# Per-head weight loads issued from GpSimd's DMA queue instead of SP's

## The chip, the cores and the metric

The kernel runs on one core of a Trainium2 chip. A core has five engines that run their own instruction streams: TensorE (PE, matrix products), VectorE (DVE), ScalarE (ACT), GpSimd (POOL) and SyncE (SP), which here only issues DMAs. An instruction waits on semaphores that other engines or finished DMAs raise, and an engine takes its instructions strictly in order. The metric is device time in microseconds (us): the median of several runs.

## The reference

`L0_attn_x` holds 2048 rows of 256 numbers. What is computed, with D = 256 and 16 heads of 128:

```python
x = x + _layernorm(attn(_layernorm(x)))
x = x + _layernorm(moe(_layernorm(x)))

# attn: every weight is codes * repeat(scales, 32, axis=0)
q, k, v = x @ wq + bq, x @ wk + bk, x @ wv + bv      # 256 -> 2048, 16 heads of 128
scores = einsum('bqhd,bkhd->bhqk', q, k) / sqrt(128)
out = einsum('bhqk,bkhd->bqhd', softmax(scores), v)
return out @ wo + bo

# moe: 8 experts of width 176, the 2 best of each row, weights renormalised
```

A weight is stored as 4-bit style codes (as float32) and one scale per 32 rows and column; the kernel multiplies the two (it "dequantizes").

## The kernel before

The attention part is one loop over `g`, which counts steps. A step is one head `h` (0 to 15) and one tile `t` (0 to 15) of 128 query rows. The instruction order on every engine is the order of the Python code (a manual schedule); the framework adds the semaphore waits.

A step makes the scores of its 128 rows against 2048 keys in two halves (`scores_half`, L447: 12 matmuls of 512 columns, operands split in a high and a low fp16 part, then a maximum on VectorE, L458). ScalarE takes the exponentials of both halves (L469), and one step later normalises them to the high part `ph` in fp16 (L483). VectorE computes the low part `pl` of what fp16 lost (L498), one half in step `g+1`, the other at the start of `g+2`. Both are 128 x 2048 and are transposed by SP-issued DMAs into `pt` (L486 for `ph`, L502 for `pl`). `ph` has three buffers, `pl` two, so a `pl` buffer comes free when its transpose has landed. TensorE multiplies `pt` with V (`pv_part`, L517 to L519) with a lag of 13 half steps, so that the products of four tiles are spread over the four steps after them.

`fill` (L538) adds, in the gaps, the projections of later Q, K and V tiles. Their results go from PSUM through ScalarE into `t32` (two buffers in turn; L204 for Q and K, L235 for V, L530 for the output of a group of four tiles), and GpSimd casts them to a high part and subtracts to get the low part (L205 and L206, L236 and L237, L531 and L532). The output tile `o` is written to HBM from GpSimd's DMA queue (L533).

Weights are handled two heads (a pair) at a time. In even heads below 14, `load_w` fetches the next pair's weights: wv at t=0, wk at t=3, wq at t=6 (L680). One load is five DMAs: four that broadcast a row of scales over 32 partitions each into `st_s` (L130, 64 KB each), and one for the codes into `st_c` (L135, 256 KB). Both staging tiles have one buffer. `dequant` (L148), at the end of steps t=2, 5 and 8, scales and multiplies on GpSimd (L152, L154). In the program's order a load stands at the very start of its step, ahead of that step's `pl` transpose (in `low_half(1)`) and `ph` transpose, all of them on SP's queue. Head 14 loads parts of `wo` instead (`load_wo`, scales from ScalarE's queue and codes from SP's).

After the loop come the output projection and the expert layers, which the change leaves alone.

Of the kernel before, what the change touches and what calls it, by code (L numbers as in the profile page):

```python
# [37 lines left out]
def sandwich(  # L38
# [22 lines left out]
    nc = tc.nc  # L61
# [53 lines left out]
    stage = proj_ctx.enter_context(tc.tile_pool(name="stage", bufs=1, side="right"))  # L115
# [4 lines left out]
    def load_w(p, which, pool, eng, sbufs=1):  # L120
        codes, scales = {
            "q": (wq_codes, wq_scales),
            "k": (wk_codes, wk_scales),
            "v": (wv_codes, wv_scales),
        }[which]
        cols = bass.ts(p, 256)
        sc = pool.tile([128, 2, 256], F32, name="st_s", bufs=sbufs)
        sv = scales.rearrange("(kc b) n -> b kc n", b=4)
        for b in range(4):
            eng.dma_start(  # L130
                out=sc[32 * b : 32 * b + 32],
                in_=sv[b : b + 1, :, cols].to_broadcast([32, 2, 256]),
            )
        cd = pool.tile([128, 2, 256], F32, name="st_c", bufs=sbufs)
        eng.dma_start(  # L135
            out=cd, in_=codes.rearrange("(kc p) n -> p kc n", p=128)[:, :, cols]
        )
        raw[(p, which)] = (sc, cd)
# [9 lines left out]
    def dequant(p, which):  # L148
        sc, cd = raw.pop((p, which))
        f = sig[:, 2, IX[which] : IX[which] + 1]  # L150
        if p > 0:
            nc.gpsimd.tensor_scalar(sc, sc, f, 1.0, ALU.mult, ALU.mult)  # L152
        w = wpool.tile([128, 2, 256], BF, name="w" + which)
        nc.gpsimd.tensor_tensor(w, cd, sc, ALU.mult)  # L154
        W[(p, which)] = w
# [18 lines left out]
    def flush():  # L174
        while pending:
            pending.pop(0)()
# [32 lines left out]
    def proj_v(p, t0, n, tag="pj", wide=None):  # L209
        w = W[(p, "v")]  # L210
        ps = proj_psum(tag)
        for j in range(n):
            i = 0
            for kc in range(2):
                for hl in range(2):
                    nc.tensor.matmul(
                        ps[:, bass.ts(j, 256)], xnT[:, t0 + j, hl * 2 + kc, :],
                        w[:, kc, :], start=(i == 0), stop=(i == 3),
                    )
                    i += 1  # L220
        if t0 % 4 == 0:
            V[(p, t0 // 4)] = kqv.tile([128, 2, 4, 256], HP, name="v", bufs=7)
        v = V[(p, t0 // 4)]
        sl = slice(t0 % 4, t0 % 4 + n)
        psv = ps[:, : n * 256].rearrange("p (t d) -> p t d", d=256)
        if wide is None:
            nc.scalar.copy(v[:, 0, sl, :], psv)
            pending.append(lambda: nc.vector.tensor_tensor(
                v[:, 1, sl, :], psv, v[:, 0, sl, :], ALU.subtract
            ))  # L230
        else:
            t32 = wide.tile([128, 512], F32, name="t32")[:, : n * 256].rearrange(
                "p (t d) -> p t d", d=256
            )
            nc.scalar.copy(t32, psv)  # L235
            nc.gpsimd.tensor_copy(v[:, 0, sl, :], t32)  # L236
            nc.gpsimd.tensor_tensor(v[:, 1, sl, :], t32, v[:, 0, sl, :], ALU.subtract)  # L237
# [209 lines left out]
    def scores_half(h, t, half, m):  # L447
        q = Q[(h, t // 4)]
        qc = bass.ts(t % 4, 128)
        s = s_pair()  # L450
        for j in range(2):
            k = K[(h, 2 * half + j)]
            nc.tensor.matmul(s[:, j, :], q[:, 0, qc], k[:, 0, :], start=True, stop=False)  # L453
            nc.tensor.matmul(s[:, j, :], q[:, 0, qc], k[:, 1, :], start=False, stop=False)  # L454
        for j in range(2):
            k = K[(h, 2 * half + j)]
            nc.tensor.matmul(s[:, j, :], q[:, 1, qc], k[:, 0, :], start=False, stop=True)  # L457
        nc.vector.tensor_reduce(m[:, half : half + 1], s, AX.XY, ALU.max)  # L458
        return s

    def negmax(m):
        nc.vector.tensor_scalar(  # L462
            m[:, 2:3], m[:, 0:1], m[:, 1:2], ssc[:, 1:2], ALU.max, ALU.mult
        )

    def softmax(pair, m):
        p = soft.tile([128, S], F32, name="p")
        for i, s in enumerate(pair):
            nc.scalar.activation(  # L469
                p[:, bass.ts(i, 1024)], s,  # L470
                AF.Exp, bias=m[:, 2:3], scale=ssc[:, 0:1], accum_out=m[:, 3 + i : 4 + i],
            )
        return p

    def recip(m):
        nc.vector.tensor_scalar(
            m[:, 5:6], m[:, 3:4], m[:, 4:5], 1.0 / PS, ALU.add, ALU.mult
        )
        nc.vector.reciprocal(m[:, 6:7], m[:, 5:6])

    def high_part(h, t, m, p):
        ph = soft.tile([128, S], HP, name="ph", bufs=3)
        nc.scalar.activation(ph, p, AF.Copy, scale=m[:, 6:7])  # L483
        if t % 4 == 0:
            PT[(h, t // 4)] = pt.tile([128, 4, 32, 128], HP, name="pt")
        nc.sync.dma_start_transpose(  # L486
            out=PT[(h, t // 4)][:, t % 4, 0:16, :], in_=ph
        )
        return ph
# [3 lines left out]
    def low_half(half, h, t, m, p, ph):  # L493
        if half == 0:
            LOW[(h, t)] = soft.tile([128, S], HP, name="pl")
        pl = LOW[(h, t)]
        cs = bass.ts(half, 1024)
        nc.vector.scalar_tensor_tensor(  # L498
            pl[:, cs], p[:, cs], m[:, 6:7], ph[:, cs], ALU.mult, ALU.subtract
        )  # L500
        if half == 1:
            nc.sync.dma_start_transpose(  # L502
                out=PT[(h, t // 4)][:, t % 4, 16:32, :], in_=LOW.pop((h, t))
            )
# [51 lines left out]
    def pv_unit(u):  # L556
        n, e = divmod(u - PVLAG, 8)
        if 0 <= n < 4 * NH:
            pv_part(n // 4, n % 4, 2 * e, 2 * e + 2)
# [68 lines left out]
    def load_oi(b, half, j, tag="kT"):  # L628
        oi = kqv.tile(
            [128, 4, 2, 256], HP, name="oi", tag=tag, bufs={"kT": 8, "v": 7}[tag]  # L630
        )
        nc.sync.dma_start(
            out=oi, in_=ot_d[b][:, 4 * j : 4 * j + 4, :, bass.ts(half, 256)]
        )
        OIN[(b, half, j)] = oi
# [40 lines left out]
    for g in range(NS + 2):  # L676
        h, t = divmod(g, NT)
        live = g < NS
        if live:
            if t in (0, 3, 6) and h % 2 == 0 and h + 2 < NH:  # L680
                load_w(h // 2 + 1, "vkq"[t // 3], stage, nc.sync)
            m = small.tile([128, 8], F32, name="m", bufs=6)
            s0 = scores_half(h, t, 0, m)
            if g == 0:
                proj_v(0, 0, 2)
                proj_v(0, 2, 2, "pv")
        if g == NS:
            load_oi(0, 1, 1)
            load_oi(0, 1, 2)
            load_oi(0, 1, 3)  # L690
        if prev is not None:
            recip(prev[2])
        if prev2 is not None:
            low_half(1, *prev2)
        flush()
        if defer:
            pv_unit(2 * g - 1)
            defer = False
        pv_unit(2 * g)
        if prev is not None:  # L700
            prev = (*prev, high_part(*prev))
        if live:
            s1 = scores_half(h, t, 1, m)
            negmax(m)
            p = softmax((s0, s1), m)
        if prev is not None:
            low_half(0, *prev)
        prev2 = prev
        first = live and (2 * g + 1 - PVLAG) % 8 == 0
        if not first:  # L710
            pv_unit(2 * g + 1)
        if live:
            fill(h, t)
        if first and h == NH - 1:
            defer = True
        elif first:
            pv_unit(2 * g + 1)
        if live:
            prev = (h, t, m, p)
        else:  # L720
            prev = None
        if h % 2 == 0 and t in (2, 5, 8) and h + 2 < NH:
            dequant(h // 2 + 1, "vkq"[t // 3])
        if h == 0 and t in (8, 9):
            tail_consts(t - 8)
        if h == NH - 2 and t in (7, 10, 13):
            load_wo((t - 7) // 3, stage, ("st_s", "st_c"), 1)
        if h == NH - 2 and t in (9, 12, 15):
            dequant_wo((t - 9) // 3)
        if h == NH - 1:  # L730
            late(t)
        if g == NS:
            X1[0] = kqv.tile([128, 4, D], F32, name="x1_0", tag="kT", bufs=8)
            nc.sync.dma_start(out=X1[0], in_=XV[:, 0])
# [440 lines left out]
```

## Time and profile before

| what | value |
|---|---|
| time, median of 3 runs | 1906.27 us (1903.36 to 1906.44) |
| profiled execution: its time / its span | 1909.43 / 1907.6 us |
| busy: PE, DVE, ACT, POOL | 94%, 86%, 72%, 44% |
| mean granted TensorE clock | 0.986 |
| DMA packets on SP's queue (q1) | 321.54 MB, 90.7% of 16 engines |
| DMA packets on GpSimd's queue (q0) | 16.81 MB, 2.9% of 16 engines |
| `load_w`, `st_s` DMAs on SP | 84 of 64 KB, about 0.42 us of issue each |
| `load_w`, `st_c` DMAs on SP | 21 of 256 KB, 0.43 us of issue each |

A group line reads: line, engine, operation, written tile <- read tiles, shapes, count, then busy time and the mean ns of one, then the idle time of the engine just before these instructions and what ended most of it. A wait line reads: engine and line that waited, who ended the wait, total us, times, longest. A timeline line reads: start, duration (us), engine, line, operation, with the idle time before it in brackets. For DMA-issuing instructions of SP the duration is that of the issue, not of the transfer.

### The profile page before, as it was taken

The numbers are of one execution on the slowest core, as the hardware profiler recorded it, in microseconds if no ns is written. First come the engines' busy times: TensorE is split into PE (matmuls) and PEld (weight loads), VectorE is DVE, ScalarE is ACT, GpSimd is POOL, SyncE is SP. The second block draws the span as 40 slices with busy tenths as digits, with TensorE's granted clock in tenths as the row PEclk, the third lists the DMA queues.
The fourth block names the chain that finished last, engine by engine and source line by source line (L and its number), as shares of the span: only waits on it lengthen the run. The fifth ranks groups of instructions, "written<-read, shape, count | busy, mean of one in ns | idle before, by whom it ended". The sixth has DMA issues, their size and how long they took to land. (4 is left out here: it accounts for less than half of the span.)

```text
span 1907.6 us, 25565 instructions
## 1 busy us (share of the span) xinstructions
PE 1799.8 (94%) x8890; PEld 936.9 (49%) x8890; DVE 1633.2 (86%) x2267; ACT 1364.7 (72%) x1730; POOL 843.4 (44%) x788
## 2 busy tenths in 40 slices
PE   7799989999999899989999899989999988899998
PEld 4344444444444344444444444434444433688887
DVE  7899979998999889988998899879999986457566
ACT  5788868887788778878887788778888776123232
POOL 2354455444544454446444544444445423233232
PEclk9999999999999999999999999999999999999999
DMA  3899999999999999999999999999999999992221
GB/s 95 171 194 190 189 184 197 191 185 189 195 191 187 180 196 190 190 185 191 196 190 184 195 194 190 178 183 192 191 188 204 212 219 216 254 241 73 60 71 56
DMA packets 1141409, 342.31 MB, mean 179 GB/s; under 512 B 1070896, under 2 KB 1131520, under 8 KB 1141280
## 3 DMA queue, kind: packets, MB, share of 16 engines
q1 hardware_dynamic: 1132960, 321.54, 90.7%
q0 software_dynamic: 5216, 16.81, 2.9%
q10 hardware_dynamic: 3104, 2.33, 0.4%
q8 instruction: 70, 1.15, 0.2%
q14 instruction: 59, 0.48, 0.1%
HBM read 53.22 MB, written 18.94 MB: 38 GB/s over the span
## 5 line engine op out<-in xcount | busy, mean ns | idle before, releaser
L498 DVE SCALAR_TENSOR_TENSOR pl<-p,m,ph 128x1024 f16<-128x1024 f32 x512 | 731.9, 1430 | 82.4 <-DMA pt<-pl 74.3
L469 ACT ACTIVATE p<-s,m,ssc 128x1024 f32<-128x1024 f32 x512 | 611.8, 1199 | 192.9 <-DVE m L462 168.1
L458 DVE TENSOR_REDUCE m<-s 128x1 f32<-128x1024 f32 x512 | 621.7, 1214 | 20.9 <-PE s L457 20.1
L483 ACT ACTIVATE ph<-p,m 128x2048 f16<-128x2048 f32 x256 | 513.0, 2004 | 116.6 <-issue 65.1
L453 PE MATMUL s<-kT,qT 128*128 128x512 f16 x1024 | 391.1, 382 | 35.6 <-ACT p L469 33.5
L518 PE MATMUL pv<-pt,v 128*128 128x512 f16 x1024 | 391.6, 382 | 31.5 <-DMA pt<-pl 30.3
L517 PE MATMUL pv<-pt,v 128*128 128x512 f16 x1024 | 391.4, 382 | 5.4 <-DMA pt<-ph 4.3
L454 PE MATMUL s<-kT,qT 128*128 128x512 f16 x1024 | 391.3, 382 | 0.0
L519 PE MATMUL pv<-pt,v 128*128 128x512 f16 x1024 | 391.1, 382 | 0.0
L457 PE MATMUL s<-kT,qT 128*128 128x512 f16 x1024 | 307.1, 382 | 0.0
L205 POOL CAST qT<-t 128x512 f16<-128x512 f32 x63 | 83.6, 1328 | 303.3 <-ACT t L204 303.3
L236 POOL CAST v<-t 128x256 f16<-128x256 f32 (+1 forms) x105 | 49.0, 466 | 304.4 <-ACT t L235 304.4
L454 PEld LDWEIGHTS <-qT 128*128 128x128 f16 x1024 | 100.5, 98 | 154.5 <-issue 53.1
L518 PEld LDWEIGHTS <-v 128*128 128x128 f16 x1024 | 100.8, 98 | 153.1 <-issue 23.8
L517 PEld LDWEIGHTS <-v 128*128 128x128 f16 x1024 | 100.9, 99 | 130.8 <-issue 7.8
L519 PEld LDWEIGHTS <-v 128*128 128x128 f16 x1024 | 100.9, 99 | 128.8 <-issue 12.9
L457 PEld LDWEIGHTS <-qT 128*128 128x128 f16 x1024 | 100.8, 98 | 123.0 <-issue 3.6
L237 POOL TENSOR_TENSOR v<-t,v 128x256 f16<-128x256 f32 (+1 forms) x105 | 155.5, 1481 | 8.4
L453 PEld LDWEIGHTS <-qT 128*128 128x128 f16 x1024 | 100.6, 98 | 111.0 <-issue 3.1
L928 POOL TENSOR_TENSOR hh<-sg,hh 128x512 fp32r<-128x512 f32 x42 | 54.5, 1297 | 144.2 <-ACT hh L927 107.6
L927 ACT CAST hh<-sg 128x512 fp32r<-128x512 f32 (+1 forms) x45 | 27.5, 611 | 118.1 <-DVE sg L939 118.0
L206 POOL TENSOR_TENSOR kT<-t,kT 128x512 f16<-128x512 f32 x60 | 104.4, 1739 | 5.1
(178 smaller groups left out, 1956.6 us busy)
## 6 DMA issues: line engine op xcount, KB each, us to landing
oi<-ot_d SPq DMA_DIRECT2D x32, 512.0 KB, 6.1
ot_d<-o POOLq DMA_DIRECT2D x63, 256.0 KB, 4.2
pt<-ph SPq DMA_TRANSPOSE x256, 5.0
pt<-pl SPq DMA_TRANSPOSE x256, 4.8
cu<-ct_d SPq DMA_DIRECT2D x16, 256.0 KB, 3.8
xt<-in_L_attn_x SPq DMA_DIRECT2D x4, 512.0 KB, 4.4
wos<-in_L_attn_wo_scales ACTq DMA_DIRECT2D x32, 64.0 KB, 4.4
woc<-in_L_attn_wo_codes SPq DMA_DIRECT2D x8, 256.0 KB, 3.4
```

Of the source, the lines that this page charges most:

```text
L206: nc.gpsimd.tensor_tensor(t[:, 1, :], t32, t[:, 0, :], ALU.subtract)
L237: nc.gpsimd.tensor_tensor(v[:, 1, sl, :], t32, v[:, 0, sl, :], ALU.subtract)
L453: nc.tensor.matmul(s[:, j, :], q[:, 0, qc], k[:, 0, :], start=True, stop=False)
L454: nc.tensor.matmul(s[:, j, :], q[:, 0, qc], k[:, 1, :], start=False, stop=False)
L457: nc.tensor.matmul(s[:, j, :], q[:, 1, qc], k[:, 0, :], start=False, stop=True)
L458: nc.vector.tensor_reduce(m[:, half : half + 1], s, AX.XY, ALU.max)
L469: nc.scalar.activation(p[:, bass.ts(i, 1024)], s, AF.Exp, bias=m[:, 2:3], scale=ssc[:, 0:1], accum_out=m[:, 3 + i : 4 + i],)
L483: nc.scalar.activation(ph, p, AF.Copy, scale=m[:, 6:7])
L498: nc.vector.scalar_tensor_tensor(pl[:, cs], p[:, cs], m[:, 6:7], ph[:, cs], ALU.mult, ALU.subtract)
L517: nc.tensor.matmul(ps, vh, d[:, :, c, :], start=(c == 0), stop=False)
L518: nc.tensor.matmul(ps, vh, d[:, :, 16 + c, :], start=False, stop=False)
L519: nc.tensor.matmul(ps, vl, d[:, :, c, :], start=False, stop=(c == 15))
```

## The change

The queue that `load_w` is given in the attention loop becomes GpSimd's. Order and positions in the program stay, so the 105 DMAs (21 loads of five) leave SP's stream and stand in GpSimd's stream at the start of steps t=0, 3 and 6 of even heads: at t=3 and t=6 right behind the `dequant` that ended the step before, and at each of the three ahead of the casts that `fill` adds in that step.

```diff
             if t in (0, 3, 6) and h % 2 == 0 and h + 2 < NH:
-                load_w(h // 2 + 1, "vkq"[t // 3], stage, nc.sync)
+                load_w(h // 2 + 1, "vkq"[t // 3], stage, nc.gpsimd)
```

`load_w` passes that queue to all its DMAs:

```python
for b in range(4):
    eng.dma_start(
        out=sc[32 * b : 32 * b + 32],
        in_=sv[b : b + 1, :, cols].to_broadcast([32, 2, 256]),
    )
...
eng.dma_start(out=cd, in_=codes.rearrange("(kc p) n -> p kc n", p=128)[:, :, cols])
```

## The prediction

> **What bounds the kernel now.** I read the page first, then busy time head by head, then the waits of SP's DMA queue, and at the end the timelines of SP, VectorE and GpSimd around single loads. From the page:
>
> ```profile
> q1 hardware_dynamic: 1132960, 321.54, 90.7%
> q0 software_dynamic: 5216, 16.81, 2.9%
> ...
> L498 DVE SCALAR_TENSOR_TENSOR pl<-p,m,ph 128x1024 f16<-128x1024 f32 x512 | 731.9, 1430 | 82.4 <-DMA pt<-pl 74.3
> ...
> ot_d<-o POOLq DMA_DIRECT2D x63, 256.0 KB, 4.2
> ```
>
> q1 is SP's queue: 512 transposes of 512 KB each fill most of it. L498 writes `pl`, which has two buffers, and waits 74.3 us for a transpose that still reads one. GpSimd's queue, q0, already carries a 256 KB store in every fourth step.
>
> A step (one head, one tile of 128 rows) starts with the first exponential, L469, so a head's length is the distance between these starts. Busy time by head, for heads 11 to 14 (columns: window, us, busy us of PE, PEld, DVE, ACT, POOL, granted clock, DMA share, GB/s):
>
> ```profile
> 1121.00:1215.30 94.30, 94.20 (x452) 44.10 (x451) 90.53 (x113) 79.85 (x100) 45.38 (x44) 1.00 1.07 189
> 1215.30:1321.90 106.60, 97.93 (x449) 44.48 (x447) 90.14 (x113) 80.05 (x99) 49.68 (x48) 0.95 1.00 184
> 1321.90:1416.20 94.30, 94.02 (x450) 43.90 (x449) 90.36 (x113) 79.79 (x100) 45.37 (x44) 1.00 1.08 190
> 1416.20:1511.30 95.10, 92.42 (x433) 42.01 (x431) 88.42 (x113) 79.02 (x95) 43.06 (x37) 1.00 1.12 204
> ```
>
> Every odd head from 1 to 13 takes 94.3 us with TensorE busy throughout. Heads 2 to 12 that carry loads do the same arithmetic (450 matmul groups against 449) and take 101.7 to 106.6, a mean of 103.24. Head 14 has no `load_w` and takes 95.1. So some 9 us of each loading head is stall.
>
> Where in the head? Mean length of the same step in heads 2, 4 ... 12 against odd heads: t=1 7.08 against 5.76, t=2 7.10 against 6.35, t=4 8.78 against 5.65, t=7 9.29 against 5.82. These four hold 1.32 + 0.75 + 3.13 + 3.47 = 8.67 of the 8.94; the other twelve hold 0.27 together. They are the steps right after the loads of t=0, 3 and 6. SP's waits say why the last two are dearest:
>
> ```profile
> SPq L130 <- POOL wv L154: 20.2, 7, 6.9
> ...
> SPq L130 <- POOL wk L154: 13.9, 6, 3.1
> ```
>
> The staging tiles have one buffer, so the load of t=3 waits until GpSimd has dequantized wv, and that of t=6 until wk is done. SP stands still meanwhile. Behind it, in order, is the transpose of a `pl` that is ready. SP's timeline at head 12, t=6:
>
> ```profile
> 1251.48 2.29 SPq L486 DMA_TRANSPOSE pt<-ph  x1
> 1256.93 1.72 SPq L130 DMA_DIRECT2D st_s<-in_L_attn_wq_scales  x4
> 1258.70 0.43 SPq L135 DMA_DIRECT2D st_c<-in_L_attn_wq_codes  x1
> 1259.22 5.14 SPq L502 DMA_TRANSPOSE pt<-pl  x1
> 1264.46 2.99 SPq L486 DMA_TRANSPOSE pt<-ph  x1
> ```
>
> VectorE finished that `pl` at 1254.35. Its transpose starts 4.87 late and its issue takes 5.14 instead of some 2. VectorE pays:
>
> ```profile
> 1261.94 0.27 DVE L462 TENSOR_SCALAR m<-m,ssc 128x1 f32<-128x1 f32 x1
> 1268.05 1.28 DVE L498 SCALAR_TENSOR_TENSOR pl<-p,m,ph 128x1024 f16<-128x1024 f32 x1 [5.84 <-DMA pt<-pl]
> ```
>
> TensorE then stands still for 4.98 us, and its next matmul rows last 0.59 us in place of 0.38; head 12's granted clock is 0.95.
>
> **The change, part by part.** It moves 7 x 3 loads of five DMAs, 105 in all, from SP to GpSimd; nothing is removed or added.
>
> *Taken from SP.* Per load 1.72 + 0.43 us of issue (2.8 where the four scale DMAs took 2.38), plus the two waits above, 34.1 us in all. The `pl` transposes then start when ready, as in head 11, where they start 0.03 to 1.19 us after VectorE, land about 5.0 after it, and the buffer is wanted again 7.0 to 7.7 after it: 2.2 us of slack. Credit: 6 heads x 8.67 = 52.0. Head 0 takes 101.3, but its first six steps also carry V projections with a VectorE subtraction; of its 7.0 I take 3.5 (ends 0 and 5). Sum 55.5.
>
> *Put on GpSimd.* Nearest row: its own store L533, 0.56 to 0.68 us of issue in 63 cases. Five make 2.8 to 3.4 us per load, 63 us over the kernel. GpSimd's queue around t=3 and t=6:
>
> ```profile
> 1239.47 0.40 POOL L236 CAST v<-t 128x256 f16<-128x256 f32 x1 [3.22 <-ACT t L235]
> ...
> 1255.63 1.27 POOL L154 TENSOR_TENSOR wk<-st_c,st_s 128x512 bf16<-128x512 f32 x1
> 1256.85 1.61 POOL L531 CAST o<-t 128x512 f16<-128x512 f32 x1
> ```
>
> At t=0 and t=3 it idles 4.13 and 3.22 us just there. At t=6 the loads stand before the casts of `o` (L531, L532), the `ot_d` store and K's casts (L205, L206). The one soon waited for is L532: ScalarE's V copy of t=7 reuses its `t32`. L532 ends 2.8 us after wk; undisturbed, that copy would come 5.9 us after the K copy of 1258.21, so 7.2 us after wk. 2.8 + 2.8 = 5.6 fits. The loads' own wait for the dequantized tile costs GpSimd nothing, as its dequant is just before them in order. Landing is not pressing: wk's load has 18 us until dequant, L533 lands in 4.2, 10.4 at worst. If GpSimd had no such idle time, each microsecond would pass to ScalarE, which is busy 79.85 of 94.3.
>
> Here the Trainium skill speaks against the change: SBUF — State Buffer, section "SBUF: two separate sides", says that descriptors of a GpSimd-issued DMA are written by GpSimd, which a VectorE operation in a two-port mode locks out; the section on the bandwidth-pool intuition gives about 620 ns alone and 3,100 ns beside such an operation. At 3.1 us a load would be 15.5 us, and the change a loss (below). L533's 0.68 at most, with VectorE over 95% busy, says that this does not happen here. I go by the row.
>
> *Returned by the DMA engines.* The bytes stay: 512 KB per load. q0's 2.9% of 1907.6 us over 64 stores is 0.86 us of all 16 engines per 256 KB, so 1.73 per load; its rows are 1 KB where the stores' are 2 KB, so at worst twice, 3.5. Against 2.2 us of slack, the delay costs 0 to 1.3 us per load. I take 0.5, nearer the lower end, since in head 11 the step with the worst store collision (landing at 7.77) lost only 0.2: 21 x 0.5 = 10.5. The skill's DMA: Bandwidth & Descriptors, section "Issuing engines are not separate DMA queues", holds that queues share the 16 engines and that issuing elsewhere saves only sequencer time, usually small. Taken as the whole effect it would leave the engines' share behind: 21 x 1.73 = 36 back, net 19. The trace goes beyond it: here the sequencer time includes waits, and head 14 moved 204 GB/s in 95.1 us, near the 207 that 19.5 MB in 94.3 us need. The engines have that room.
>
> *Sum.* -55.5 + 10.5 = -45.0. Profiled span 1907.6 to 1862.6, its own time 1909.43 to 1864.4. The median of the runs is 3.2 below that execution: 1906.27 - 45.0 = 1861.3.
>
> **The rivals.**
> 1. *The engines decide* (0.19). Transposes and loads now interleave, and a transpose in flight loses the load's 1.73 us every time. For: DMA share 1.0 everywhere. Against: head 14. 55.5 - 36.3 = 19 gained, 1887.
> 2. *Slower: GpSimd is held up while issuing* (0.09), at t=6. With x us per DMA, the V copy waits 5x + 2.8 - 7.2, less ScalarE's 0.9 of slack. At 3.1 that is 10.2 per head, 71 over seven heads, 26 more than gained: 1932. It decides from 5x = 5.3 + 45/7 = 11.7, so x = 2.3 us. For: the skill's rule, and GpSimd's own 128x512 subtractions, which stretch from 1.16 to 2.0. Against: L533.
> 3. *No change* (0.05): the late transposes come from the loads' bytes alone, and wait as long in another queue: 1906. Against: the two queue waits, and stalls that are dearest where SP waited longest.
>
> **How the numbers follow.** The likeliest case (0.67) is 1861, its own range 1849 (no return, head 0 in full) to 1876 (1.3 us per load is 27 back, less a little). Upwards the range takes in rival 1: 1847 to 1890. 0.2%, 4 us, is about what a measurement here can tell from no change. Faster: 0.67 + 0.19 = 0.86; same 0.05; slower 0.09.
>
> **What would show it.** SP's waits on wv and wk gone; heads 2 to 12 between 94.5 and 97 us; L498's wait for `pt` down from 74 to under 30; 105 GpSimd issues at 0.5 to 0.7 us; q0 near 28 MB. Right in direction but too hopeful: steps t=1, 4 and 7 still 1 to 2 us long, with L502 issues of 3 to 5 us. Wrong: issue rows of 2 us or more on GpSimd, ScalarE waiting at L235 or L204, steps t=7 and 8 longer than before.

## The result, and the profile after

The changed kernel takes 1881.57 us (median of 4 runs, 1879.05 to 1886.2), the kernel before 1904.82 beside it. The ratio is 0.9884, 95% interval 0.9856 to 0.9913: 17 to 27 us faster. The forecast was 1861 with a range of 1847 to 1890. The direction and the range held, and about half of the forecast gain came. The profiled execution has a span of 1877.3 us.

The page of the changed kernel, the lines that answer to those shown of before:

```profile
q1 hardware_dynamic: 1120528, 310.53, 90.4%
q0 software_dynamic: 9584, 27.82, 5.9%
...
L498 DVE SCALAR_TENSOR_TENSOR pl<-p,m,ph 128x1024 f16<-128x1024 f32 x512 | 731.6, 1429 | 50.2 <-DMA pt<-pl 43.9
...
ot_d<-o POOLq DMA_DIRECT2D x63, 256.0 KB, 4.1
```

11 MB have gone from SP's queue to GpSimd's. VectorE's wait for a `pl` transpose fell from 74.3 to 43.9 us; the forecast had said under 30. Of these 43.9 us, 22.8 stand in heads 14 and 15 (21.6 before), which have no `load_w`. In heads 0 to 13 the wait fell from 52.7 to 21.1 us.

Busy time of heads 11 to 14 of the changed kernel (window, us, busy us of PE, PEld, DVE, ACT, POOL, granted clock, DMA share, GB/s):

```profile
1096.20:1190.50 94.30, 93.92 (x450) 43.79 (x448) 90.38 (x113) 79.84 (x100) 46.32 (x46) 1.00 1.06 190
1190.50:1291.30 100.80, 95.84 (x450) 43.89 (x448) 90.12 (x113) 80.14 (x99) 59.30 (x62) 0.98 1.11 193
1291.30:1385.60 94.30, 93.92 (x450) 43.77 (x448) 90.37 (x113) 79.80 (x100) 45.37 (x44) 1.00 1.07 190
1385.60:1483.00 97.40, 94.25 (x433) 42.48 (x431) 88.62 (x113) 78.91 (x96) 41.55 (x37) 0.98 1.10 200
```

Odd heads are where they were. Head 12 fell from 106.6 to 100.8; heads 2 to 12 that carry loads have a mean of 98.73 in place of 103.24, not the 94.5 to 97 forecast. Head 14, which the change does not touch, moved from 95.1 to 97.4 and head 15 back by as much, so single heads are good to some 2 us.

The dear steps also changed places. Mean length in heads 2, 4 ... 12 (before, after, odd heads): t=4 8.78, 5.84, 5.65; t=7 9.29, 6.15, 5.82. Those two are nearly cured. But t=5 went from 5.76 to 6.82 and t=8 from 5.66 to 7.45. So the stall behind SP's wait is gone, and a smaller one, one step later, has come.

SP no longer waits for the dequant. GpSimd, whose waits follow (engine and line, who ended it, total us, times, longest), waits 0.3 us for its own instruction:

```profile
POOL st_s L130 <- POOL wv L154: 2.1, 7, 0.3
POOL st_s L130 <- POOL wk L154: 2.1, 7, 0.3
```

GpSimd's timeline at the load of t=3 in head 12, then SP's at the same time:

```profile
1211.86 2.21 POOL L130 DMA_DIRECT2D st_s<-in_L_attn_wk_scales  x4 [0.30 <-POOL wv L154]
1214.06 0.73 POOL L135 DMA_DIRECT2D st_c<-in_L_attn_wk_codes  x1
1214.79 0.94 POOL L236 CAST v<-t 128x256 f16<-128x256 f32 x1
```

```profile
1210.29 1.79 SPq L502 DMA_TRANSPOSE pt<-pl  x1
1212.18 4.85 SPq L486 DMA_TRANSPOSE pt<-ph  x1
1217.12 4.61 SPq L502 DMA_TRANSPOSE pt<-pl  x1
1221.82 2.06 SPq L486 DMA_TRANSPOSE pt<-ph  x1
```

Issuing costs GpSimd 2.94 us per load, as forecast. But the two transposes in flight beside the load take 4.85 and 4.61 us to issue, where two together take 4.89 on average in the odd heads of this kernel. That is 4.6 us longer for the two, and VectorE waits:

```profile
1222.42 0.28 DVE L462 TENSOR_SCALAR m<-m,ssc 128x1 f32<-128x1 f32 x1
1223.94 1.28 DVE L498 SCALAR_TENSOR_TENSOR pl<-p,m,ph 128x1024 f16<-128x1024 f32 x1 [1.24 <-DMA pt<-pl]
```

### The profile page after: what moved, and what is told of

Same layout as the page of the kernel before. It is cut to its first block, busy times and chain, and to the rows that moved or that the text cites. A ratio compares the mean times of both kernels' runs of the same rounds, so it can differ in the third digit from the quotient of the medians.

```text
span 1877.3 us, 25533 instructions
## 1 busy us (share of the span) xinstructions
PE 1794.1 (96%) x8890; PEld 936.0 (50%) x8890; DVE 1632.4 (87%) x2267; ACT 1365.5 (73%) x1730; POOL 907.5 (48%) x893
## 5 line engine op out<-in xcount | busy, mean ns | idle before, releaser
L498 DVE SCALAR_TENSOR_TENSOR pl<-p,m,ph 128x1024 f16<-128x1024 f32 x512 | 731.6, 1429 | 50.2 <-DMA pt<-pl 43.9
L236 POOL CAST v<-t 128x256 f16<-128x256 f32 (+1 forms) x105 | 54.3, 517 | 271.8 <-ACT t L235 271.8
L237 POOL TENSOR_TENSOR v<-t,v 128x256 f16<-128x256 f32 (+1 forms) x105 | 146.8, 1398 | 8.4
```

The costliest lines, as they stand in the source:

```text
L498: nc.vector.scalar_tensor_tensor(pl[:, cs], p[:, cs], m[:, 6:7], ph[:, cs], ALU.mult, ALU.subtract)
```

## The experiments

After the result, the theory is: SP's wait was worth what was gained, and the rest is DMA engine time that loads take from transposes, whichever queue they are on. Rivals for the rest: GpSimd's issue time and the casts behind it; the dequants beside VectorE; SP's issue time and in-order queue. Twelve runs; gains and losses are worked out as (ratio - 1) x 1906 us, each ratio against the kernel before on the same chip.

**The wait taken away, the queue kept.** Two ways: a load a whole step after the dequant that frees its tiles, or in the same step but behind both transposes.

```diff
-            if t in (0, 3, 6) and h % 2 == 0 and h + 2 < NH:
-                load_w(h // 2 + 1, "vkq"[t // 3], stage, nc.sync)
+            if t in (0, 4, 8) and h % 2 == 0 and h + 2 < NH:
+                load_w(h // 2 + 1, "vkq"[t // 4], stage, nc.sync)
...
-        if h % 2 == 0 and t in (2, 5, 8) and h + 2 < NH:
-            dequant(h // 2 + 1, "vkq"[t // 3])
+        if h % 2 == 0 and t in (2, 6, 10) and h + 2 < NH:
+            dequant(h // 2 + 1, "vkq"[t // 4])
```

> Loads stay on SP's queue, but stand at t=0, 4 and 8 in place of 0, 3 and 6, and the dequants at the end of t=2, 6 and 10 in place of 2, 5 and 8: each load of wk and wq comes a whole step after the dequant that frees its staging tiles, so SP never waits for GpSimd. SP's own issue time (about 2.2 us per load) and all bytes stay on its queue. Theory A (the gain of the change is the removed wait of SP for the dequant; what is left is the bytes): like the changed kernel, 1876 to 1886. Theory B (SP's issue time and its in-order queue cost as much as the wait): 1890 to 1900.

```diff
-            if t in (0, 3, 6) and h % 2 == 0 and h + 2 < NH:
-                load_w(h // 2 + 1, "vkq"[t // 3], stage, nc.sync)
...
             prev = (*prev, high_part(*prev))
+        if live and t in (0, 3, 6) and h % 2 == 0 and h + 2 < NH:
+            load_w(h // 2 + 1, "vkq"[t // 3], stage, nc.sync)
```

> The loads stay on SP's queue in the same steps, but stand behind that step's two transposes in place of ahead of them. The dequant that frees the tiles is done by then, so SP does not wait for it, and the ready pl transpose no longer stands behind a load. If the removed wait is the gain: 1876 to 1888, like the changed kernel and like the loads a step later. If the place ahead of the transposes also costs: under 1870.

Measured: 1886.5, ratio 0.9908 (0.989 to 0.9926), and 1886.63, 0.9914 (0.9883 to 0.9946). SP's waits for the two dequants, 34.1 us before, are gone in both. What is left of waits at the scale DMAs is 3.2 us in the first run and 5.5 in the second, for other instructions. The longest of the first run:

```profile
SPq L130 <- POOL v L237: 3.0, 5, 1.0
```

Both gain 16 to 18 us with no load leaving SP. So most of the change's 22 us comes with the removed wait. Both edits also change which transposes a load meets, and the next run shows that this can weigh as much. That two different places agree speaks for the wait, and so do the steps: with the loads in the same steps as before but behind the transposes, t=4 takes 5.72 and t=7 6.00, against 5.84 and 6.15 in the changed kernel. The intervals overlap that of the changed kernel a little, so whether the other queue adds something on top these two cannot say.

**The same places, the other queue.** From the first of these two, only the queue changes:

```diff
-                load_w(h // 2 + 1, "vkq"[t // 4], stage, nc.sync)
+                load_w(h // 2 + 1, "vkq"[t // 4], stage, nc.gpsimd)
```

> Loads at t=0, 4 and 8 and dequants at t=2, 6 and 10, as in the run that kept SP's queue at these places (1886.5), but on GpSimd's queue: the queue is the only difference to that run, and neither waits for a dequant. If the waits were the whole gain of the change: 1880 to 1888. If a queue of its own is worth something: 1875 or less.

Measured: 1904.43 (10 runs, 1885.72 to 1913.51), ratio 0.996 (0.9932 to 0.9988). Both expectations missed: at these places GpSimd's queue is 10 us *worse* than SP's, and it scatters over 28 us. Moving the loads a step later gains 17 us on SP's queue and moving them to GpSimd's queue gains 22, but both together gain only 8. SP's timeline in head 10, steps t=8 and 9, right behind the load of t=8, and busy time before, beside and after it:

```profile
1065.14 5.46 SPq L486 DMA_TRANSPOSE pt<-ph  x1
1070.69 9.39 SPq L502 DMA_TRANSPOSE pt<-pl  x1
1080.18 2.98 SPq L486 DMA_TRANSPOSE pt<-ph  x1
```

```profile
1056.00:1064.00 8.00, 8.00 (x43) 4.02 (x41) 7.72 (x10) 6.27 (x8) 4.66 (x5) 1.00 1.12 171
1066.00:1080.00 14.00, 7.96 (x39) 3.63 (x37) 8.63 (x13) 10.51 (x14) 9.31 (x11) 0.93 1.16 94
1080.00:1088.00 8.00, 4.92 (x12) 1.73 (x13) 1.29 (x1) 0.00 (x0) 2.21 (x3) 0.50 1.18 241
```

The last two columns are the point. The DMA share counts the time that packets are under way. For 14 us it is as high as ever (1.16), and the engines move 94 GB/s in place of 171; once the load is through, 241. They are not short of work, they are slow. Counted from the packet records of this trace (SP's packets are nearly all transposes):

```
stretch      GpSimd queue         SP queue
us           packets  KB  mean ns packets  KB   mean ns
1058-1060       0     -    -       1502   376    22
1066-1068      55    132  226       573   141    25
1072-1074      18     56  585       360    90    80
1078-1080       8     20  208       390    96    96
1084-1086       0     -    -       1787   439    20
```

A transpose's packet of 256 bytes takes 20 to 22 ns alone in these stretches. Beside the load it takes 25 ns in the first 2 us and later 80 to 96. Why it slows only then is open. In the changed kernel the same is milder. Its busy time before, beside and after the load of t=3 in head 12:

```profile
1206.00:1214.00 8.00, 8.00 (x40) 3.82 (x39) 7.03 (x10) 5.42 (x9) 6.79 (x8) 1.00 1.10 186
1214.00:1222.00 8.00, 8.00 (x39) 3.63 (x38) 7.52 (x10) 6.91 (x7) 4.17 (x6) 1.00 1.08 154
1222.00:1230.00 8.00, 6.93 (x35) 3.23 (x34) 6.66 (x10) 6.14 (x9) 4.96 (x5) 1.00 1.18 229
```

The rate falls beside a load on SP's own queue too. The kernel before, at the load of t=6 in head 12:

```profile
1256.90:1264.90 8.00, 8.00 (x43) 3.99 (x41) 5.24 (x7) 6.58 (x11) 5.11 (x6) 1.00 0.70 97
```

It moves 97 GB/s, but with a share of 0.70: SP has just come out of its wait, and the engines partly lack work. A low rate alone is therefore no sign of slow packets; the share has to be read beside it.

**No loads at all, and issues without bytes.** Both keep one codes tile loaded once, and both dequant instructions; the second adds five 4 KB DMAs on GpSimd at each place.

```diff
-                load_w(h // 2 + 1, "vkq"[t // 3], stage, nc.sync)
+                load_keep(h // 2 + 1, "vkq"[t // 3], n)      # n = 0 or 5
...
+    def load_keep(p, which, n):
+        if not KEEP: ...                                     # one 256 KB codes tile, once
+        sc = stage.tile([128, 2, 256], F32, name="st_s", bufs=1)
+        cd = KEEP[0]
+        for i in range(n):
+            nc.gpsimd.dma_start(out=cd[:, 0, 8 * i : 8 * i + 8],
+                                in_=wq_codes[0:128, 256 + 8 * i : 264 + 8 * i])
+        raw[(p, which)] = (sc, cd)
...
-            nc.gpsimd.tensor_scalar(sc, sc, f, 1.0, ALU.mult, ALU.mult)
+            nc.gpsimd.tensor_scalar(sc, cd, f, 0.01, ALU.mult, ALU.mult)
```

> No load at all after a first codes tile: every dequant of the pairs 1 to 7 still runs on GpSimd, with the same two instructions, on one codes tile that stays (scales are left out and the weights are wrong from head 2 on). Floor for the loads' cost. If the loads are all that makes loading heads longer: heads 2 to 12 at 94.3 to 94.8 us, total 1848 to 1854. If the dequants beside VectorE are what is left in the changed kernel (4.4 us per loading head): 1872 to 1880.

> GpSimd issues five DMAs of 4 KB at each place of a load and nothing else (weights come from one codes tile that stays, scales are left out). GpSimd's issue time without the bytes. If issue time and the casts behind it count: 1865 to 1880. If only the bytes count: within 4 us of the run without loads, 1840 to 1850.

Measured: 1842.79, ratio 0.9671 (0.9655 to 0.9687), and 1843.73, 0.9684 (0.9653 to 0.9716). Two rivals fall. The dequants cost nothing: heads 2 to 12 take 92.98 us with them, below an odd head. And 105 more issues on GpSimd, 2.7 us for each five and with the casts waiting behind them, add 2.5 us by the two ratios; the far ends of the intervals leave room for 12. Head 12 without loads:

```profile
1165.40:1258.30 92.90, 92.81 (x447) 43.56 (x445) 89.15 (x113) 79.96 (x100) 54.54 (x48) 1.00 1.08 192
```

TensorE is busy for all but 0.1 us. So the loads cost the kernel before 62.7 us in all, and the change removed 22 of them.

**Half of the bytes.** Codes alone and scales alone, both on GpSimd's queue at the changed kernel's places. The load leaves out its scale DMAs in the first and its codes DMA in the second, and `dequant` makes up for what is not there:

```diff
# codes alone
-        for b in range(4):
+        for b in range(0 if only_codes else 4):
...
-            nc.gpsimd.tensor_scalar(sc, sc, f, 1.0, ALU.mult, ALU.mult)
+            nc.gpsimd.tensor_scalar(sc, cd, f, 0.01, ALU.mult, ALU.mult)
...
-                load_w(h // 2 + 1, "vkq"[t // 3], stage, nc.sync)
+                load_w(h // 2 + 1, "vkq"[t // 3], stage, nc.gpsimd, only_codes=True)
# scales alone: load_keep is load_w without its last DMA, and cd is None
-        nc.gpsimd.tensor_tensor(w, cd, sc, ALU.mult)
+        nc.gpsimd.tensor_tensor(w, sc, sc, ALU.mult) if cd is None else nc.gpsimd.tensor_tensor(w, cd, sc, ALU.mult)
...
-                load_w(h // 2 + 1, "vkq"[t // 3], stage, nc.sync)
+                load_keep(h // 2 + 1, "vkq"[t // 3], stage, nc.gpsimd)
```

> The loads on GpSimd's queue as in the changed kernel, but only the codes DMA of each (256 KB in place of 512 KB, one issue of 0.73 us in place of five of 2.9 us); the scales are left out (the dequant multiplies the codes by themselves). Theory A (what is left is DMA engine time that loads take from transposes, with some slack): less than half of the 31 us that are left, 1850 to 1862. If dequants are what is left: 1875 to 1882.

> Only the four scale DMAs of each load on GpSimd's queue (256 KB in four DMAs of 32 partitions); the codes are left out, the dequant squares the scales. Theory A1 (size of the burst): as with codes alone, 1844 to 1852. Theory A2 (scale DMAs are the dear ones): 1868 to 1882.

Measured: 1847.55, ratio 0.9694 (0.9676 to 0.9713), and 1854.46, 0.9745 (0.9715 to 0.9775). Above the run without loads that is 4 us (within the intervals, so perhaps nothing) and 14 us for 256 KB each, where both together cost 40. The halves do not add up to the whole, as theory A expected; that a small load fits into slack would explain it. But the scales are dearer than the same bytes of codes, which it did not say.

**All of the bytes, spread.** The codes DMA one step after the scale DMAs (part 0 of `load_w_part` issues the four scale DMAs, part 1 the codes DMA):

```diff
-            if t in (0, 3, 6) and h % 2 == 0 and h + 2 < NH:
-                load_w(h // 2 + 1, "vkq"[t // 3], stage, nc.sync)
+            if t in (0, 1, 3, 4, 6, 7) and h % 2 == 0 and h + 2 < NH:
+                load_w_part(h // 2 + 1, "vkq"[t // 3], stage, nc.gpsimd, t % 3)
```

> The changed kernel with each load in two halves a step apart, all on GpSimd's queue: the four scale DMAs at t=0, 3 and 6, the codes DMA at t=1, 4 and 7. Same DMAs, same bytes, same issue time, never more than 256 KB at once. Theory A1 (a burst of 512 KB outruns the slack that a transpose has, one of 256 KB does not, as with codes alone): 1844 to 1856. Theory A2 (it is the four scale DMAs, their broadcast or their number, that slow the transposes): 1870 to 1882.

Measured: 1874.3, ratio 0.9861 (0.9826 to 0.9896). A1 falls: bursts of 256 KB a step apart are not free. The time lies in A2's range, but A2 does not stand either: the scales alone took 1854.46 where it said 1868 to 1882. Then thinner still, one DMA of 64 or 128 KB per step, in 18 of 32 steps, once from each queue:

```diff
-            if t in (0, 3, 6) and h % 2 == 0 and h + 2 < NH:
-                load_w(h // 2 + 1, "vkq"[t // 3], stage, nc.sync)
+            pt_ = t + 16 * (h % 2)
+            if h < NH - 2 and pt_ < 24 and pt_ % 8 < 6:
+                load_piece(h // 2 + 1, "vkq"[pt_ // 8], stage, nc.gpsimd, pt_ % 8)
...
-        if h % 2 == 0 and t in (2, 5, 8) and h + 2 < NH:
-            dequant(h // 2 + 1, "vkq"[t // 3])
+        if h < NH - 2 and t + 16 * (h % 2) in (7, 15, 23):
+            dequant(h // 2 + 1, "vkq"[(t + 16 * (h % 2)) // 8])
```

> All bytes kept and all on GpSimd's queue, but spread thin: one DMA of 64 KB (scales) or 128 KB (half of the codes) per step, six steps per load, over steps 0 to 5, 8 to 13 and 16 to 21 of the 32 steps of a pair of heads; dequants two steps behind each. Complete result. If what is left in the changed kernel is the rate at which load bytes meet the transposes in a few steps: 1843 to 1858, near the run without loads. If the bytes cost the same wherever they stand (no spare room on the DMA engines at all): 1870 to 1882.

> The same thin spread from SP's queue. SP never waits for a dequant, and spends about 0.45 us of issue in 18 of 32 steps. If the queue does not matter once the waits are gone: within 6 us of the thin spread on GpSimd's queue. If SP's issue time or its in-order queue matters by itself: 10 us or more slower than that.

Measured on GpSimd's queue: 1874.86, ratio 0.9827 (0.9797 to 0.9856). By its ratio it is the fastest version here that loads everything, about 11 us better than the changed kernel, with intervals that just touch. It still stands 30 us above the run without loads, and in the range of the second expectation: thin spreading saves a quarter of the 40 us, and most of the bytes' cost stays.

On SP's queue: 1909.94, ratio 1.0009 (0.9988 to 1.003), no gain at all. This run does not test what its expectation says, because of a flaw in it: a dequant ends step 7 and the next load's first DMA opens step 8, so SP waits for the dequant as in the kernel before. Its waits (L155 and L179 are this kernel's numbers of L130 and L154):

```profile
SPq L155 <- POOL wv L179: 24.9, 6, 5.1
SPq L155 <- POOL wk L179: 17.5, 7, 2.9
```

Read so, it is useful: on GpSimd's queue, behind the very same dequants, the same bytes at the same places take 35 us less. The queue differs between the two runs and not the wait alone, but the step lengths point at the wait. Over a pair of heads SP's run is 6.4 us longer; t=9 and t=10 of the even heads, behind the wait for wv, are 4.8 us longer, and t=1 to t=3 of the odd heads, behind the wait for wk, 2.6. All other steps together are 1.0 us shorter.

**ScalarE's queue.** From the kernel before:

```diff
-                load_w(h // 2 + 1, "vkq"[t // 3], stage, nc.sync)
+                load_w(h // 2 + 1, "vkq"[t // 3], stage, nc.scalar)
```

> The same loads, same places in the program, on ScalarE's DMA queue: GpSimd issues nothing, and the bytes still have a queue of their own beside the transposes. ScalarE then waits for the dequant of wv and wk at t=3 and t=6 and spends its own sequencer time. Theory A (bytes on the DMA engines are what is left): not under 1876, and up to 1900 with the waits of ScalarE. If the changed kernel's rest came from GpSimd's issue time or from its software queue: 1860 or less, unless ScalarE's own waits show at L130.

Measured: 1953.6, ratio 1.0259 (1.0242 to 1.0276), slower than either expectation. ScalarE's timeline at t=3 of head 12:

```profile
1265.90 0.68 ACT L204 ACTIVATE t<-pj,bqs 128x512 f32<-128x512 f32 x1
1271.39 1.76 ACTq L130 DMA_DIRECT2D st_s<-in_L_attn_wk_scales  x4
1273.19 0.44 ACTq L135 DMA_DIRECT2D st_c<-in_L_attn_wk_codes  x1
1273.74 2.00 ACT L483 ACTIVATE ph<-p,m 128x2048 f16<-128x2048 f32 x1 [7.15 <-issue]
```

ScalarE waits for the dequant, which stands on GpSimd behind a cast of what ScalarE has just written (L204). Steps t=2 and t=5 take 12.2 and 11.9 us. It is the same wait as SP's, on an engine that is itself busy for 80 us of each head. At t=0, where nothing is waited for, the load costs next to nothing (t=0 and t=1 take 5.63 and 5.59, as without loads, and t=15 before it 6.05 in place of 5.82); whether that queue suits the bytes better stays open.

**What makes the scales dear.** The changed kernel, with scale DMAs that read 32 rows of codes in place of one scale row broadcast to 32 partitions (and a factor of 0.01 in `dequant`):

```diff
-        sv = scales.rearrange("(kc b) n -> b kc n", b=4)
+        sv = codes.rearrange("(kc p) n -> p kc n", p=128)
...
-                in_=sv[b : b + 1, :, cols].to_broadcast([32, 2, 256]),
+                in_=sv[32 * b : 32 * b + 32, :, cols],
```

> The changed kernel with one thing different: the four scale DMAs read 32 different rows of the codes in place of one row of scales broadcast to 32 partitions. Same number of DMAs, same bytes, same destination, same queue and places (the weights are wrong from head 2 on). With codes alone the run took 1847.6, with scales alone 1854.5, so the scale DMAs are the dearer half. If the broadcast read makes them dear: 1850 to 1866. If only bytes and number of DMAs count: 1876 to 1886, like the changed kernel.

Measured: 1869.81, ratio 0.9799 (0.9765 to 0.9833), between the two expectations and clear of the changed kernel's interval. So reading a broadcast row accounts for some 16 of the 40 us (the intervals leave 4 to 28), and not for the rest. The rows read here are those that the codes DMA of the same load reads too; whether that makes them cheap was not tested.

**The runs on GpSimd's queue together.** q0's share of 16 engines times the span, less that of the run without loads (3.1% of 1845.6 us), over 21 loads, is the engine time of a load's packets. Beside it the time that a load costs above the run without loads:

| run | engine time of a load, us | cost of a load, us |
|---|---|---|
| five DMAs of 4 KB | 0.3 | 0.1 |
| codes alone | 0.8 | 0.2 |
| scales alone | 1.4 | 0.7 |
| thin | 2.0 | 1.4 |
| no broadcast | 2.2 | 1.2 |
| spread over two steps | 2.4 | 1.7 |
| changed kernel | 2.6 | 1.9 |
| a step later | 2.9 | 2.6 |

The cost grows with the engine time, except between "thin" and "no broadcast", and is some 0.1 to 1.0 us less than it. The packets are themselves slowed by the transposes, so this is a relation, not a proof of which comes first.

## Why the prediction was right or wrong

- *The number*: it lies in the stated range because that range took in the first rival. The likeliest case's own range, 1849 to 1876, does not hold it (its low end comes out as 1847 from its own terms, 1906.27 - 52.0 - 7.0). Two errors partly cancel: the credit was 7 us too small and the return 30 too small.
- *The wait on SP, and the transposes behind it*: right. The runs that keep SP's queue and take the wait away gain 16 to 18 us, and thin loads with the wait, on SP's queue, take 35 us more than without it on GpSimd's. The two steps it was read from, t=4 and t=7, are nearly cured.
- *The credit of 55.5*: right in kind and small by 7. The loads cost 62.7 in all. The floor was taken from odd heads at 94.3, but an even head without loads takes 92.98.
- *GpSimd's issue*: right. Measured issues are 0.53 to 0.67 us for scales and 0.73 to 0.75 for codes, and five small issues per load cost nothing that is clear of noise. The prediction quotes the Trainium skill (SBUF — State Buffer, section "SBUF: two separate sides") on descriptors that a two-port VectorE operation locks out. Such a lock would have made the change a loss, and it does not show here: no issue takes over 0.76 us, with VectorE 89 to 96% busy. Whether any VectorE operation of this kernel runs in such a mode no trace says, so the rule itself was not tested; and the page's 3,100 ns are the time of a whole DMA, where the prediction took them for an issue. Of the signs named for "wrong", step t=8 did become longer than before (7.45 against 5.66), but without the others: no long issue, and ScalarE waits at L235 once, for 0.4 us.
- *Returned by the DMA engines, 10.5*: **this step failed**. It is 40 (34 to 47 with the intervals), or 1.9 us per load in place of 0.5. Three readings in it were off. The engine time per load is 2.6 us and not 1.73: taken from the store of `o`, it left out the dearer scale DMAs (1.4 us by themselves, the codes 0.8). It was inside the "at worst" of 3.5. The cost is that time less 0.7 us, not less 2.2. A likely reason, read from one load: the slack was taken from transposes late one at a time, while a load delays a `ph` and a `pl` transpose one after the other (4.85 + 4.61 against 4.89). And head 14's 204 GB/s was taken as proof of room. It is a mean over a head, and says nothing of the stretch in which loads and transposes mix, where the rate falls to 154 and once to 94. Yet head 14 leaves something open: it carries three loads of 512 KB itself (parts of `wo`, at the end of t=7, 10 and 13), and TensorE is busy for 92.42 of its 95.10 us (94.25 of 97.40 in the changed kernel). So there a load costs about 1 us of TensorE's time at most. What makes it cheaper, the queues or the place, was not tested.
- *The rival "the engines decide", 1887*: nearer to the truth than the likeliest case. That loads take DMA engine time from the transposes is what the runs point to, and its 36 us returned are close to the 40. That they are so close is in part luck: it took 1.73 us of engine time with no slack, and the runs show 2.6 with 0.7 of slack. It was given 0.19 because of head 14.

The 40 is what is left of 62.7 after the 22 gained; no run measures it by itself.

## What to carry to other kernels

In a queue that runs in order, look for the DMA that waits for another engine: it delays every ready transfer behind it. Here moving it within its queue (a step later, or behind the others) gained 16 to 18 us and moving it to another queue 22, but the two do not add: both at once gained 8. Then price the bytes separately, since moving a load to another queue leaves them where they were; take their price from stretches in which both kinds of transfer run, not from the mean rate of a stage. A load that waits did best here on the engine that makes what it waits for, where order already serves the wait; from ScalarE's queue the kernel was 49 us slower than before.

## What the runs showed of the hardware

- Plain loads on one queue slow the transposes on another by more than their bytes: at two loads shown the total rate falls from 186 to 154 GB/s, and from 171 to 94 over 14 us, with the DMA share above 1 throughout. In the second, packets of transposes go from 20 to 22 ns to 80 to 96.
- Small loads can be nearly free beside the same transposes (256 KB of codes: 0.2 us each; 256 KB of scales: 0.7) and larger ones were not (512 KB: 1.9 us), even cut into one piece per step (1.4 us).
- A source row broadcast to 32 partitions cost more than 32 rows that another DMA of the load reads too: some 16 us over 84 DMAs of 64 KB. Why is open.
- The place of a load can matter much: loads at t=0, 4 and 8 (with their dequants moved along) in place of 0, 3 and 6, on GpSimd's queue, cost 14 us and scatter over 28 us from run to run, though on SP's queue the same move gained 17. Why the two queues differ so is open.
